# Attention mask: from a matmul into the score bank to a product after the exponential, with the sums one stage later

## The chip, the core and the metric

The kernel runs on one core of one Trainium2 chip. The metric is device time in microseconds (us) for one call; lower is better. One core has TensorE (matrix multiplies; PE in the profile, with its weight loads as PEld), VectorE (DVE), ScalarE (ACT), GpSimd (POOL), and DMA queues, here issued mostly by SyncE (SP). Every engine works through its own list of instructions in a fixed order and waits at an instruction until what it needs is there.

## The reference, cut to what matters

`y = scan_block(x, cond)` for 32 sequences of 256 tokens with 256 features, then two attention and feed-forward layers on `y`, then `x + result`. The part that the change touches is the local attention of each layer (8 heads of 64, window 128, so a sequence has two windows):

```python
sim  = jnp.einsum('bhwid,bhwjd->bhwij', bq, bk)          # q is already scaled
mask = (i < j) | (i > j + WINDOW) | (j == -1)
sim  = jnp.where(mask, -jnp.finfo(sim.dtype).max, sim)
attn = jax.nn.softmax(sim, axis=-1)
out  = jnp.einsum('bhwij,bhwjd->bhwid', attn, bv)
```

A masked score has weight zero; the rest is the exponential divided by its sum over the keys. Queries and keys are normalised to unit length, so the scores are bounded, and the kernel takes the exponential without subtracting a maximum (a second program in the file, for scales where that is not safe, is not run here).

## The kernel before

There are two kinds of work. The **scan** goes over the 256 tokens of eight sequences at a time (four groups): each of its 1024 steps is one custom VectorE instruction `h<-h,xrep,lim` (L660) that adds a scaled row to a state of 128x512 and clips it; TensorE reads the states out (`y`, L672), ScalarE scales the rows (`xrep`, L650), and chunks of 32 tokens have their own projection, convolution (`acc`, L442 on VectorE, first tap L431 on GpSimd), normalisation and output. The **attention and feed-forward** work goes over 64 items, one for each group, layer and sequence, in that order.

The two run side by side. For item n the program writes its steps into numbered stages, eight for an item (`ST = 8`); stage i of item n is entry 8n+i, and an entry of 8 or more falls into the time of the following items. The loop at the end emits the entries in order, and after each of them the scan steps that are due (`scan_to`): two for an entry, so one chunk of 32 scan steps goes with two items. A scheduler of the language then orders the instructions of each engine from this; `tc.keep_in_program_order` pins some of them. After the fourth group's scan has ended only attention and feed-forward are left.

What an item does, with the lines of the profile:

- `project` (L907): q, k, v of a window, two matmuls of 128x512 each; `rotated` works on q and k: square on ScalarE (L920), two products and a sum on VectorE (L923, L928, L933, L937), and on GpSimd an addition (L931), a power (L939) and a product (L940). This is done for the following item.
- `turn` (L946): transposes of q and k into `qT` and `kT`.
- `scores`: for keys of window `kw` and `n` pairs of heads, two PSUM banks `sc` of 128x512 (r is the head of the pair). Keys are the partitions, queries the columns. A bf16 matmul of an identity with a mask of 0 and -32768 (L1106) opens each bank; the score matmuls (L1113) accumulate onto it. ScalarE then writes the exponential into a tile `pT` (L1122; six buffers). Three calls an item: all four pairs against the second window's keys (`kw` 1, stage 2), and twice two pairs against the first window's keys (`kw` 0, stages 3 and 5). So an item has six banks, six mask matmuls and six exponentials.
- `sums` (L1132): the sums of `pT` over keys, 16 matmuls into one bank `rs`, and a reciprocal on VectorE (L1140). `values` (L1151): 16 matmuls of `pT` with `v_sb`, copied by ScalarE into `oT` (L1158). Both in stage 7.
- `put_inverse`, `load_inverse`: the reciprocal goes to DRAM and comes back spread over partitions (SyncE queue); `divide` multiplies `oT` with it (L1175); `finish` projects out (L957) and adds to the residual `res` (L965).
- `feed`: normalise (L1193 to L1203), `apply` (L1210), `spread` (L1223), `widen` (L1246, with a GELU L1254 on ScalarE), `product` (`ag`, L1262), `narrow` (L1274, with L1285).
- `fetch`: at the end of a layer the weights of the next one, on the SyncE queue.

All PSUM tiles are one rotation of eight banks (tag "w").

Of the kernel before, what the change touches and what calls it, by code (L numbers as in the profile page):

```python
# [10 lines left out]
FP = mybir.dt.float32  # L11
BF = mybir.dt.bfloat16
I32 = mybir.dt.int32
AF = mybir.ActivationFunctionType
ALU = mybir.AluOpType
# [4 lines left out]
P = 128  # L20
# [18 lines left out]
W = 128  # L39
# [4 lines left out]
LN_EPS = 1e-5  # L44
CLIP = 10.0
MASKED = -1e30
MASKED_LOW = -32768.0


SCALES2 = 25.0  # L50
# [2 lines left out]
def bc(ap, axis, n):  # L53

    ap = ap.unsqueeze(axis)
    shape = list(ap.shape)
    shape[axis] = n
    return ap.broadcast_to(shape)
# [15 lines left out]
def kernel(  # L74
# [29 lines left out]
    nc = tc.nc  # L104
# [4 lines left out]
    const = ctx.enter_context(tc.tile_pool(name="const", bufs=1))  # L109
# [35 lines left out]
    ident = const.tile([P, P], FP, tag="ident", name="ident")  # L145
# [17 lines left out]
    for j in range(NJ):  # L163
# [9 lines left out]
    nc.gpsimd.memset(half, 0.5)  # L173

    mask_t = const.tile([P, 2 * W], BF, tag="mask_t", name="mask_t")
    ident_b = const.tile([P, P], BF, tag="ident_b", name="ident_b")
    nc.vector.tensor_copy(ident_b, ident)
    nc.gpsimd.memset(mask_t, 0.0)  # L180
    nc.gpsimd.affine_select(
        out=mask_t[:, 0:W], in_=mask_t[:, 0:W], compare_op=ALU.is_ge, fill=MASKED_LOW,
        base=0, pattern=[[1, W]], channel_multiplier=-1,
    )
    nc.gpsimd.affine_select(
        out=mask_t[:, W : 2 * W], in_=mask_t[:, W : 2 * W], compare_op=ALU.is_ge,
        fill=MASKED_LOW, base=0, pattern=[[-1, W]], channel_multiplier=1,
    )

    head_cols = const.tile([P, 2, 32], FP, tag="head_cols", name="head_cols")  # L190
# [28 lines left out]
    def program(ctx, exact):  # L219
# [9 lines left out]
        ps_w = ctx.enter_context(tc.tile_pool(name="psw", bufs=8, space=PSUM, reuse_waits="tile"))  # L229
# [737 lines left out]
        if exact:  # L967

            mask = rpool.tile([P, 2 * W], FP, tag="mask", name="mask")
            nc.gpsimd.memset(mask, 0.0)  # L970
            nc.gpsimd.affine_select(
                out=mask[:, 0:W], in_=mask[:, 0:W], compare_op=ALU.is_ge, fill=MASKED,
                base=0, pattern=[[1, W]], channel_multiplier=-1,
            )
            nc.gpsimd.affine_select(
                out=mask[:, W : 2 * W], in_=mask[:, W : 2 * W], compare_op=ALU.is_ge, fill=MASKED,
                base=0, pattern=[[-1, W]], channel_multiplier=1,
# [94 lines left out]
        class Attention:  # L1072
# [2 lines left out]

            def __init__(self, l):
                self.l = l
                self.qkv, self.rot, self.p, self.o = {}, {}, {}, {}

            def project(self, b, w, a):  # L1080
                if w == 0 and a == 2:
# [16 lines left out]
            def scores(self, b, kw, i0, n):  # L1098


                qT, kT, _ = self.qkv[b]
                nq = S - kw * W
                banks = []
                for r in range(2):
                    sc = ps_w.tile([P, n, nq], FP, tag="w", name="sc")
                    nc.tensor.matmul(  # L1106
                        sc, ident_b, bc(mask_t[:, 0:nq], 1, n), start=True, stop=False
                    )
                    banks.append(sc)
                for i in range(n):  # L1110
                    for r in range(2):
                        rows = slice(r * DH, (r + 1) * DH)
                        nc.tensor.matmul(  # L1113
                            banks[r][:, i, :],
                            kT[rows, i0 + i, kw * W : (kw + 1) * W],
                            qT[rows, i0 + i, kw * W :],
                            start=False,
                            stop=(i == n - 1),
                        )
                for r in range(2):  # L1120
                    p = aw.tile([P, n, nq], FP, tag="pT", name="pT", bufs=6)
                    nc.scalar.activation(p, banks[r], AF.Exp)  # L1122
                    for i in range(n):
                        self.p[b, kw, i0 + i, r] = p[:, i, :]

            def sums(self, b):

                rs = bank(ps_w, "w", "rs")[:, 0:S]
                for kw in range(NW):
                    for r in range(2):  # L1130
                        for i in range(HEADS // 2):
                            nc.tensor.matmul(  # L1132
                                rs[32 * i : 32 * i + 32, kw * W :],
                                head_cols[:, r],
                                self.p[b, kw, i, r],
                                start=(kw == 0 and r == 0),
                                stop=(kw == NW - 1 and r == 1),
                            )
                rinv = aw.tile([P, S], FP, tag="rinv", name="rinv", bufs=1)
                nc.vector.reciprocal(rinv, rs)  # L1140
                self.rinv = rinv
# [155 lines left out]
        if exact:  # L1297
            for g in range(NG):
# [4 lines left out]
                for l in range(L):  # L1303
# [4 lines left out]
                    for b in range(GB):  # L1308
                        ff = FeedForward(g, l, b)
# [18 lines left out]
        def stage(n, i, what, *args):  # L1328
            stages.setdefault(ST * n + i, []).append(partial(what, *args))

        def attend(n, at, b, nxt):

            stage(n, 0, at.turn, b, 1)
            stage(n, 3, at.scores, b, 0, 0, 2)
            stage(n, 2, at.scores, b, 1, 0, HEADS // 2)
            stage(n, 5, at.scores, b, 0, 2, 2)
            stage(n, 7, at.sums, b)
            stage(n, 7, at.values, b)
            stage(n + 1, 0, at.put_inverse)
            stage(n + 1, 2, at.load_inverse)  # L1340
            stage(n + 1, 4, at.divide, b)
            stage(n + 1, 6, at.finish, b)
            if nxt is not None:
                for w in range(NW):
                    for i, a in ((0, 2), (1, 0), (1, 1)):
                        stage(n, 3 * w + i, nxt[0].project, nxt[1], w, a)
                stage(n, 6, nxt[0].turn, nxt[1], 0)

        def feed(n, g, l, b):
            ff = FeedForward(g, l, b)  # L1350
            for w in range(NW):
                stage(n + 1, 8 + w, ff.normalise, w)
                stage(n + 2, 1 + w, ff.apply, w)
                stage(n + 2, 2 + w, ff.spread, w)
            for m in range(NM):
                stage(n + 2, 4 + m, ff.widen, m)
                stage(n + 2, 5 + m, ff.product, m)
            for d in range(KM):
                stage(n + 3, 3 + d, ff.narrow, d)

        def fetch(n, g, l, b):

            if b == GB - 1 and (g, l) != (NG - 1, L - 1):
                nl = (l + 1) % L
                for i, a in ((5, 2), (6, 0), (6, 1)):
                    stage(n - 1, i, load_weights, nl, "qkv", a)
                stage(n + 2, 0, load_weights, nl, "wo")
                for m in range(NM):
                    stage(n + 2, 6 + m, load_weights, nl, "w1", m)
                stage(n + 3, 6, load_weights, nl, "w2")  # L1370
            if l == L - 1 and g < NG - 1:
                stage(n + 6, 2, load_res, g + 1, b)

# [2 lines left out]
        for n, (g, l, b) in enumerate(seqs):  # L1376
            nxt = (ats[n + 1], seqs[n + 1][2]) if n + 1 < len(seqs) else None
            attend(n, ats[n], b, nxt)
            feed(n, g, l, b)
        for n, (g, l, b) in enumerate(seqs):  # L1380
            fetch(n, g, l, b)
# [22 lines left out]
        for t in range(max(stages) + 1):  # L1404
# [3 lines left out]
            g, r = divmod(t + 1 + group - reload, group)  # L1408
# [10 lines left out]
    with tc.If(fits > 0) as which:  # L1419
        with ExitStack() as es:  # L1420
            program(es, False)
    with which.Else():
        with ExitStack() as es:
            program(es, True)
# [81 lines left out]
def _program(ins, out_shape):  # L1506
    import concourse.bacc as _bacc

    nc = _bacc.Bacc("TRN2", target_bir_lowering=False, num_devices=1)
    arrays, args = {}, []  # L1510
    for name, a in ins.items():
        arrays[f"in_{name}_dram"] = a
        args.append(
            nc.dram_tensor(
                f"in_{name}_dram", a.shape, mybir.dt.from_np(a.dtype), kind="ExternalInput"
            ).ap()
        )
    args.append(nc.dram_tensor("out_0_dram", out_shape, FP, kind="ExternalOutput").ap())
    with tile.TileContext(nc) as tc:
        kernel(tc, *args)  # L1520
    return nc, arrays
# [11 lines left out]
```

## Time and profile before

| | |
|---|---|
| time, median of 3 runs | 3769.12 us (3767.9 to 3770.96) |
| profiled execution, its own time | 3770.68 us |
| its span in the trace | 3768.9 us |
| granted TensorE clock, mean | 0.986 |
| busy in the span: PE / PEld | 3644.0 us (97%) / 2255.5 us (60%) |
| DVE / ACT / POOL | 2639.5 us (70%) / 2163.9 us (57%) / 1796.0 us (48%) |
| last scan step starts at | 2928.3 us |
| first mask matmul starts at | 515.1 us |

The span is the execution as the trace shows it; the profiled execution's own time is 1.8 us more than the span, and 1.6 us above the median. Busy time is a sum over the whole span, so an engine that is busy for 97% of it can still be waiting for another one in one stretch and be the limit in another. The first 480 us are scan alone; from there to about 2,930 us scan and attention run together; the last 840 us have no scan.

### The profile page before, as it was taken

Reading aid. Unit: us, or ns where it says so; the run is one execution under the profiler, and the core shown is the slowest. Engines: PE = TensorE matmul, PEld = TensorE weight load, DVE = VectorE, ACT = ScalarE, POOL = GpSimd, SP = SyncE. Lnnn points to the kernel's source line nnn. Section 1 sums busy time; section 2 is a strip of 40 time slices with the busy share of each in tenths; the row PEclk is TensorE's granted clock in tenths of the full one; section 3 lists DMA queues with packets and bytes.
Section 4 is the critical chain, followed back from the end, with each engine's and each line's share of the span. In section 5 each row is a group of like instructions: output and inputs, shape, how many; then the busy total and the mean of one; then the engine's idle time right before and its main releaser. Section 6 shows DMA issues by size and latency. Waiting matters only on the chain.

```text
span 3768.9 us, 57035 instructions
## 1 busy us (share of the span) xinstructions
PE 3644.0 (97%) x20028; PEld 2255.5 (60%) x20028; DVE 2639.5 (70%) x5177; ACT 2163.9 (57%) x3769; POOL 1796.0 (48%) x1776
## 2 busy tenths in 40 slices
PE   7999989999999999999999999999999999999998
PEld 3333345666666666666666666666666666666666
DVE  6988888788778777777777777777776444444443
ACT  3555556666666666656666665666566444444442
POOL 4443365544455455545445555545454444433441
PEclk8999999999999999999999999999999999999999
DMA  5444555344454545444444545444353111011101
GB/s 149 114 119 117 135 155 135 101 119 116 116 130 123 145 120 150 106 108 114 112 120 110 147 119 138 115 101 116 108 130 109 54 43 50 12 29 38 29 26 35
DMA packets 396250, 387.53 MB, mean 103 GB/s; under 512 B 176355, under 2 KB 256052, under 8 KB 395828
## 3 DMA queue, kind: packets, MB, share of 16 engines
q1 hardware_dynamic: 311506, 371.80, 37.1%
q10 hardware_dynamic: 84450, 12.01, 2.0%
q8 instruction: 161, 2.64, 0.3%
q14 instruction: 133, 1.09, 0.1%
HBM read 348.05 MB, written 34.08 MB: 101 GB/s over the span
## 4 chain that ended last, share of the span: by engine, by line
PE 68%; DVE 16%; POOL 6%; ACT 4%; issue 3%; DMA 3%; SPq 0%; ACTq 0%; POOLq 0%; DVEq 0%
PE ps_qkv L907 14%; PE pa L1246 13%; PE po_f L1274 8%; PE y L672 5%; DVE h L660 5%; PE ps_wo L957 4%; PE sc L1113 4%; PE ov L1151 3%; DVE acc L442 3%; PE ps_out L750 3%; PE ps_in L395 3%; PE tr_qk L946 2%; POOL rn L939 2%; PE rs L1132 2%; PE sc L1106 2%
## 5 line engine op out<-in xcount | busy, mean ns | idle before, releaser
L660 DVE CUSTOM_DVE_ANT_0 h<-h,xrep,lim 128x512 f32<-128x512 f32 x1024 | 936.5, 915 | 238.7 <-ACT xrep L650 207.7
L907 PE MATMUL ps_qkv<-qkv,res 128*128 128x512 f32 x1536 | 712.1, 600 | 23.6 <-DVE ag L1262 18.2
L650 ACT ACTIVATE xrep<-xrep,beta 128x512 f32<-128x512 f32 x896 | 622.5, 717 | 113.2 <-DMA xrep<-xnd 71.0
L1246 PE MATMUL pa<-hT,w 128*128 128x256 f32 (+1 forms) x3072 | 684.4, 385 | 0.3 <-DVE zT L741 0.2
L1246 PEld LDWEIGHTS pa<-hT,w 128*128 128x128 f32 (+1 forms) x3072 | 498.4, 178 | 159.6 <-issue 44.1
L931 POOL TENSOR_TENSOR rot<-rot,swp 128x512 f32<-128x512 f32 x256 | 335.2, 1309 | 368.9 <-DVE swp L928 223.7
L939 POOL TENSOR_TENSOR rn<-ss,neg_half 128x8 f32<-128x8 f32 x256 | 460.3, 1798 | 17.8 <-DVE ss L937 7.9
L907 PEld LDWEIGHTS ps_qkv<-qkv,res 128*128 128x128 f32 x1536 | 278.0, 191 | 300.5 <-issue 260.5
L1274 PE MATMUL po_f<-ag,w 128*128 128x256 f32 (+1 forms) x1536 | 386.8, 393 | 13.5 <-DVE ag L1262 8.9
L1203 POOL TENSOR_TENSOR rstd<-ve,neg_half 128x1 f32<-128x1 f32 x128 | 81.2, 634 | 645.7 <-DVE ve L1201 642.8
L672 PE MATMUL y<-h,ly 128*32 128x512 f32 x2048 | 372.7, 620 | 10.6 <-DVE h L660 9.8
L1274 PEld LDWEIGHTS po_f<-ag,w 128*128 128x128 f32 (+1 forms) x1536 | 273.0, 189 | 120.0 <-issue 54.6
L1262 DVE SCALAR_TENSOR_TENSOR ag<-pa,b_sb,ag 128x256 f32<-128x256 f32 (+1 forms) x448 | 212.5, 474 | 171.6 <-ACT ag L1254 168.0
L940 POOL TENSOR_TENSOR rot<-rot,rn 128x512 f32<-128x512 f32 x256 | 301.1, 1176 | 20.0
L1254 ACT ACTIVATE ag<-pa,b_sb 128x256 f32<-128x256 f32 x320 | 150.7, 471 | 268.1 <-PE pa L1246 266.0
L395 PE MATMUL ps_in<-xg,w_in_sb 128*128 128x256 f32 x1024 | 282.8, 407 | 19.1 <-DMA xg<-in_xT_dram 14.9
L920 ACT ACTIVATE sq<-ps_qkv 128x512 f32<-128x512 f32 x256 | 151.7, 596 | 236.5 <-PE ps_qkv L907 200.1
L395 PEld LDWEIGHTS ps_in<-xg,w_in_sb 128*128 128x128 f32 x1024 | 189.9, 198 | 142.4 <-issue 41.2
L442 DVE SCALAR_TENSOR_TENSOR acc<-xr,wc_sb,acc 128x256 f32<-128x256 f32 x384 | 189.5, 496 | 91.7 <-POOL acc L431 89.6
L923 DVE TENSOR_TENSOR rot<-ps_qkv,rc_sb 128x512 f32<-128x512 f32 x256 | 175.3, 685 | 82.9 <-ACT sq L920 82.9
L957 PE MATMUL ps_wo<-oT,wo 128*128 128x256 f32 x1024 | 231.6, 379 | 0.0
L450 ACT ACTIVATE th<-acc 128x256 f32<-128x256 f32 x128 | 53.0, 414 | 308.3 <-DVE acc L442 255.0
(146 smaller groups left out, 5672.4 us busy)
## 6 DMA issues: line engine op xcount, KB each, us to landing
xrep<-xnd SPq DMA_DIRECT2D x896, 256.0 KB
rb<-inv SPq DMA_DIRECT2D x128, 256.0 KB
xnd<-xn SPq DMA_DIRECT2D x64, 256.0 KB
qkv<-in_wqkv_dram SPq DMA_DIRECT2D x24, 512.0 KB
xd<-xnd SPq DMA_DIRECT2D x192, 64.0 KB
w<-in_w_dram SPq DMA_DIRECT2D x80, 128.0 KB
xg<-in_xT_dram SPq DMA_DIRECT2D x64, 128.0 KB
ys<-yo ACTq DMA_DIRECT2D x64, 128.0 KB
```

The costliest lines, as they stand in the source:

```text
L395: nc.tensor.matmul(ps, w_in_sb[:, k, ch * P : (ch + 1) * P], ck[c]["xg"][:, k], start=(k == 0), stop=(k == KM - 1),)
L442: nc.vector.scalar_tensor_tensor(acc, xr[:, :, k : k + CH], wc_sb[:, ch, k : k + 1], acc, ALU.mult, ALU.add,)
L650: scaled = nc.scalar.activation(bx, ck[c].pop(("bx", t), bx), AF.Copy, scale=ck[c]["beta"][:, t : t + 1])
L660: nc.vector._custom_dve(TENSOR_ADD_SAT, out=h_new, in0=state["h"], in1=bx, s0=ck[c]["lim"][:, 0, t : t + 1], s1=ck[c]["lim"][:, 1, t : t + 1],
L672: nc.tensor.matmul(ck[c]["y", hb][32 * q : 32 * q + 32, :], ly[hb % 2][:, 32 * t : 32 * t + 32], ck[c].pop(("h", hb * TB + t)), start=(i = ...
L907: nc.tensor.matmul(ps, res[b][:, k, t0 : t0 + W], wt["qkv", a][:, k], start=(k == 0), stop=(k == KM - 1),)
L931: nc.gpsimd.tensor_add(rot, rot, swp)
L939: nc.gpsimd.tensor_tensor(rn, ss, neg_half, ALU.pow)
L940: nc.gpsimd.tensor_mul(rot, rot, bc(rn, 2, DH))
L957: nc.tensor.matmul(po[:, d], wt["wo", 0][:, c, d * P : (d + 1) * P], oT[:, c, :], start=(c == 0), stop=(c == NC_ - 1),)
L1246: nc.tensor.matmul(pg if x else pa, wt["w1", m][:, k, x], self.h[:, k], start=(k == 0), stop=(k == KM - 1),)
L1274: nc.tensor.matmul(self.po[:, d], wt["w2", 0][r0 : r0 + n, m, d * P : (d + 1) * P], self.ag[m][r0 : r0 + n], start=(m == 0), stop=(m == le ...
```

## The change

The mask matmuls (`ident_b`, bf16 `mask_t`) are left out; each score matmul writes its own columns. `mask_t` becomes a float32 tile of ones and zeros, and a new step `mask` multiplies each `pT` tile of 128x512 in place with it: on GpSimd for `kw` 1 (two products an item, stage 3), on VectorE for `kw` 0 (two in stage 4 and two in stage 6). Each product is pinned in program order. `sums` and `values` move from stage 7 of an item to stage 0 of the following one, and all that comes after them for the item (the inverse's two transfers, divide, finish, the feed-forward steps, the fetches of wo, w1 and w2) moves by one stage too. The qkv fetches and the loading of the next group's residual stay.

```diff
--- before.py
+++ after.py
@@ -44,7 +44,6 @@
 LN_EPS = 1e-5
 CLIP = 10.0
 MASKED = -1e30
-MASKED_LOW = -32768.0
 
 
 SCALES2 = 25.0
@@ -173,18 +172,15 @@
     nc.gpsimd.memset(half, 0.5)
 
 
-
-    mask_t = const.tile([P, 2 * W], BF, tag="mask_t", name="mask_t")
-    ident_b = const.tile([P, P], BF, tag="ident_b", name="ident_b")
-    nc.vector.tensor_copy(ident_b, ident)
-    nc.gpsimd.memset(mask_t, 0.0)
+    mask_t = const.tile([P, 2 * W], FP, tag="mask_t", name="mask_t")
+    nc.gpsimd.memset(mask_t, 1.0)
     nc.gpsimd.affine_select(
-        out=mask_t[:, 0:W], in_=mask_t[:, 0:W], compare_op=ALU.is_ge, fill=MASKED_LOW,
+        out=mask_t[:, 0:W], in_=mask_t[:, 0:W], compare_op=ALU.is_ge, fill=0.0,
         base=0, pattern=[[1, W]], channel_multiplier=-1,
     )
     nc.gpsimd.affine_select(
         out=mask_t[:, W : 2 * W], in_=mask_t[:, W : 2 * W], compare_op=ALU.is_ge,
-        fill=MASKED_LOW, base=0, pattern=[[-1, W]], channel_multiplier=1,
+        fill=0.0, base=0, pattern=[[-1, W]], channel_multiplier=1,
     )
 
     head_cols = const.tile([P, 2, 32], FP, tag="head_cols", name="head_cols")
@@ -1075,7 +1071,7 @@
 
             def __init__(self, l):
                 self.l = l
-                self.qkv, self.rot, self.p, self.o = {}, {}, {}, {}
+                self.qkv, self.rot, self.p, self.ps, self.o = {}, {}, {}, {}, {}
 
             def project(self, b, w, a):
                 if w == 0 and a == 2:
@@ -1102,11 +1098,7 @@
                 nq = S - kw * W
                 banks = []
                 for r in range(2):
-                    sc = ps_w.tile([P, n, nq], FP, tag="w", name="sc")
-                    nc.tensor.matmul(
-                        sc, ident_b, bc(mask_t[:, 0:nq], 1, n), start=True, stop=False
-                    )
-                    banks.append(sc)
+                    banks.append(ps_w.tile([P, n, nq], FP, tag="w", name="sc"))
                 for i in range(n):
                     for r in range(2):
                         rows = slice(r * DH, (r + 1) * DH)
@@ -1114,14 +1106,25 @@
                             banks[r][:, i, :],
                             kT[rows, i0 + i, kw * W : (kw + 1) * W],
                             qT[rows, i0 + i, kw * W :],
-                            start=False,
-                            stop=(i == n - 1),
+                            start=True,
+                            stop=True,
                         )
                 for r in range(2):
                     p = aw.tile([P, n, nq], FP, tag="pT", name="pT", bufs=6)
                     nc.scalar.activation(p, banks[r], AF.Exp)
+                    self.ps[kw, i0, r] = p
                     for i in range(n):
                         self.p[b, kw, i0 + i, r] = p[:, i, :]
+
+            def mask(self, kw, i0):
+
+                e = nc.gpsimd if kw else nc.vector
+                for r in range(2):
+                    p = self.ps.pop((kw, i0, r))
+                    n, nq = p.shape[1:]
+                    tc.keep_in_program_order(
+                        e.tensor_mul(p, p, bc(mask_t[:, 0:nq], 1, n))
+                    )
 
             def sums(self, b):
 
@@ -1334,12 +1337,15 @@
             stage(n, 3, at.scores, b, 0, 0, 2)
             stage(n, 2, at.scores, b, 1, 0, HEADS // 2)
             stage(n, 5, at.scores, b, 0, 2, 2)
-            stage(n, 7, at.sums, b)
-            stage(n, 7, at.values, b)
-            stage(n + 1, 0, at.put_inverse)
-            stage(n + 1, 2, at.load_inverse)
-            stage(n + 1, 4, at.divide, b)
-            stage(n + 1, 6, at.finish, b)
+            stage(n, 3, at.mask, 1, 0)
+            stage(n, 4, at.mask, 0, 0)
+            stage(n, 6, at.mask, 0, 2)
+            stage(n + 1, 0, at.sums, b)
+            stage(n + 1, 0, at.values, b)
+            stage(n + 1, 1, at.put_inverse)
+            stage(n + 1, 3, at.load_inverse)
+            stage(n + 1, 5, at.divide, b)
+            stage(n + 1, 7, at.finish, b)
             if nxt is not None:
                 for w in range(NW):
                     for i, a in ((0, 2), (1, 0), (1, 1)):
@@ -1349,14 +1355,14 @@
         def feed(n, g, l, b):
             ff = FeedForward(g, l, b)
             for w in range(NW):
-                stage(n + 1, 8 + w, ff.normalise, w)
-                stage(n + 2, 1 + w, ff.apply, w)
-                stage(n + 2, 2 + w, ff.spread, w)
+                stage(n + 1, 9 + w, ff.normalise, w)
+                stage(n + 2, 2 + w, ff.apply, w)
+                stage(n + 2, 3 + w, ff.spread, w)
             for m in range(NM):
-                stage(n + 2, 4 + m, ff.widen, m)
-                stage(n + 2, 5 + m, ff.product, m)
+                stage(n + 2, 5 + m, ff.widen, m)
+                stage(n + 2, 6 + m, ff.product, m)
             for d in range(KM):
-                stage(n + 3, 3 + d, ff.narrow, d)
+                stage(n + 3, 4 + d, ff.narrow, d)
 
         def fetch(n, g, l, b):
 
@@ -1364,10 +1370,10 @@
                 nl = (l + 1) % L
                 for i, a in ((5, 2), (6, 0), (6, 1)):
                     stage(n - 1, i, load_weights, nl, "qkv", a)
-                stage(n + 2, 0, load_weights, nl, "wo")
+                stage(n + 2, 1, load_weights, nl, "wo")
                 for m in range(NM):
-                    stage(n + 2, 6 + m, load_weights, nl, "w1", m)
-                stage(n + 3, 6, load_weights, nl, "w2")
+                    stage(n + 2, 7 + m, load_weights, nl, "w1", m)
+                stage(n + 3, 7, load_weights, nl, "w2")
             if l == L - 1 and g < NG - 1:
                 stage(n + 6, 2, load_res, g + 1, b)
```

## The prediction

> **What bounds the kernel now.** I read the page's busy row and chain first, then the groups for prices, then the chain in order of time over one repetition of the work, then a table of windows cut where that chain changes engine.
>
> ```profile
> PE 3644.0 (97%) x20028; PEld 2255.5 (60%) x20028; DVE 2639.5 (70%) x5177; ACT 2163.9 (57%) x3769; POOL 1796.0 (48%) x1776
> PE 68%; DVE 16%; POOL 6%; ACT 4%; issue 3%; DMA 3%; SPq 0%; ACTq 0%; POOLq 0%; DVEq 0%
> ```
>
> PE is busy for 97%, yet carries only 68% of the chain. So there is time in which PE is busy and still not what sets the end. The page's groups price the products' neighbours; the answers for single lines give minimum, median and maximum.
>
> ```profile
> L660 DVE CUSTOM_DVE_ANT_0 h<-h,xrep,lim x1024: 707/810/1919, 54.3 to 2928.3; 128x512 f32<-128x512 f32 x171
> L923 DVE TENSOR_TENSOR rot<-ps_qkv,rc_sb x256: 672/683/694, 488.0 to 3666.8; 128x512 f32<-128x512 f32 x128
> L1175 DVE TENSOR_TENSOR oT<-oT,rb x64: 1214/1215/2291, 568.9 to 3724.0; 128x1024 f32<-128x1024 f32 x64
> L931 POOL TENSOR_TENSOR rot<-rot,swp x256: 1259/1272/1723, 489.4 to 3670.5; 128x512 f32<-128x512 f32 x128
> ```
>
> The chain repeats every two items (one chunk of the scan): the same `po_f` pair after a PE wait stands at 1543.69 and at 1652.26, 108.57 us apart. From 1543.69 to 1611.75 it is PE without a gap. Then it leaves PE (excerpt):
>
> ```profile
> 1610.02 1.73 PE ps_qkv L907 x4
> 1611.77 0.60 ACT sq L920
> 1612.40 0.69 DVE rot L923
> ...
> 1619.42 2.05 POOL rn L939
> ...
> 1622.55 1.27 POOL xd L702
> 1623.82 0.55 POOL acc L431
> 1624.39 0.48 DVE acc L442
> ...
> 1651.82 0.39 DVE ag L1262
> 1652.22 0.04 issue
> 1652.26 0.70 PE po_f L1274 x2
> 1652.96 0.37 PE tp_hn L1223 x2
> 1653.33 0.43 PE sc L1106 x2
> ```
>
> ```profile
> 1543.69:1611.75 68.06, 68.06 (x373) 43.44 (x374) 47.80 (x86) 42.36 (x75) 34.07 (x27) 1.00 0.44 114
> 1611.75:1652.26 40.51, 38.60 (x244) 25.32 (x244) 33.60 (x77) 25.20 (x44) 20.10 (x27) 1.00 0.32 85
> 2900.00:3300.00 400.00, 400.00 (x2270) 266.74 (x2269) 185.13 (x387) 192.27 (x311) 175.82 (x147) 1.00 0.15 41
> ```
>
> The columns are window, length, then busy PE, PEld, DVE, ACT, POOL. Of 108.57 us, 68.06 are a **PE stretch** (PE 100%, DVE 70%) and 40.51 a **VectorE stretch**: the convolution and the decays of the next chunk meet the rotations, DVE is busy for 33.60 us (83%), and PE idles only 1.91 us, because it has almost as much work. There a shorter PE gains nothing, and VectorE's time is the chain. In the last 840 us, without scan, PE is at 100% and DVE at 46%: the pure PE case.
>
> **What the Trainium skill says.** "SBUF — State Buffer", section "Who interferes with whom": a VectorE instruction with two SBUF inputs contends with a GpSimd instruction that reads SBUF, one with a single SBUF input does not. The trace agrees: `h` (two SBUF inputs) spreads from 707 to 1919 ns with a mean of 915, `rot` (one input from PSUM) stays within 672 to 694. Both new products have two SBUF inputs. "VectorE: DVE Perf Modes", the errata section, gives (N+151)/0.96 ns for a float32 tensor_tensor: 691 ns for 512 elements, and 1224 for 1024, where `oT` has 1215. "GPSIMD Engine Reference", "Engine selection", has two-input work about twice as slow on GpSimd: here 1272 against 683 ns.
>
> **The change part by part.**
>
> *Mask matmuls out.* The chain has 0.43 us for a pair, so 0.215 us each. Six an item, 64 items: 384 x 0.215 = 82.6 us of PE. Answers for L1106 by window find 128 of them after 2800 us, 250 from 560 to 2800, 6 before. After 2800 the chain is PE alone: 128 x 0.215 = **-27.5 us**, on the path. In a repetition, four pairs lie in the PE stretch (1544.76, 1561.93, 1595.83, 1600.71): -1.72 us; two lie in the VectorE stretch (1616.77, 1647.70): nothing. Their weight loads (98 ns) lie beside matmuls; nothing.
>
> *Products on VectorE*, 256 of 128x512. Not in the trace of before; bounded by 0.60 us (back-to-back `rot` in the chain) and 0.92 (`h`'s contended mean). I take 0.70, the skill's 691 ns. Per repetition eight, in four pairs. Two fall in the PE stretch, where DVE has 20 us to spare: nothing. The changed kernel's instruction order, as built, has the third just before the first `rot` of the VectorE stretch, where VectorE idled 0.81 and 1.35 us and where `divide` (1.22 us) moves away, to behind `zT`, into VectorE's 3.06 us wait for `acc` L431: nothing. It has the fourth between the `acc` steps that follow, where VectorE is the chain: +1.40 us. The repetition: -1.72 + 1.40 = -0.32. There are 250/12 = 20.8 of them: **-6.7 us**. If the cover is gone, each pair adds 1.2 to 1.84.
>
> *The new waits.* A product waits for its exponential. Queued behind it on VectorE are `h`, `acc` and `rot`, and all that waits for them; in the old trace the exponential of the fourth pair ends at 1619.8 and the place is about 1625, so I take no wait. Bounds: 0 to the 1.28 us table load before an exponential.
>
> *Products on GpSimd*, 128 of about 1.27 us, two an item at stage 3, so 2.5 us; behind them stand the rotations of the second window, for which `turn` waits. GpSimd was idle for 10.7 us before 1613.9, and without scan the last L940 ends at 3632.9 and its transposes begin at 3641.9: nothing. They do lock out `h` and the VectorE products while they run; from nothing up to 2.5 us for a repetition, if one pair meets the VectorE stretch. I take nothing, as the built order has them ahead of it.
>
> *One stage later.* `sums` comes three stages after its last exponential instead of two, so the product fits: 8 us lay between at 3627.6 to 3635.6, and 1.4 are needed. All its followers keep their spacing: the reciprocal, put_inverse and load_inverse (three DMAs an item on SP, each now behind about two more `xrep` loads in that queue, and SP waits there for the reciprocal as before), divide, finish. At seven layer ends 15 weight DMAs (wo, twelve w1, two w2) move by a stage too, with a stage of 5 to 7 us; their tiles come free as much later, so they are as far from their use. The v copy that reuses the buffer follows `values` on PE anyway; `pT` buffers come free more than 10 us before the next exponential of `kw` 1 needs them. All nothing. Only head and tail count: one stage without followers at the head, and one more of them at the end. A stage without scan is 41.57/8 = 5.2 us (the item period, 3607.93 to 3649.50); PE does the same work, so between 0 and 5.2: **+3 us**.
>
> Sum: -27.5 - 6.7 + 3 = -31.2. Against the profiled execution's 3770.68: 3739.5. That execution stands 1.56 above the median of the runs, so **3738 us**.
>
> **The rivals.**
>
> *PE limits everywhere* (the VectorE stretch dissolves because the work is realigned by a stage): 82.6 - 3 off, 3690. For it: PE's 97%. Against: 40 of every 108 us have their chain elsewhere.
>
> *The VectorE stretch grows* and the kernel is slower. Place: 1611 to 1652. Price: the third pair finds no idle time, both contended: 2 x 1.84 = 3.68, and the reciprocal (1751 ns), which ran beside a ScalarE chain at 1635.9 and stands a stage later in the new order, before `st` and `rot` that close the stretch: 1.75. Growth 5.43, less 1.72, times 20.8: +77; with -27.5 + 3: 3822. It decides from (27.5 - 3)/20.8 + 1.72 = 2.9 us of growth. For it: VectorE at 83% there with GpSimd locking; against: waits of 2 to 3 us in it that can absorb.
>
> *No change*: growth near 2.9, one pair and most of the reciprocal: 3769.
>
> *It does not do what it says*: the built order has 256 products on VectorE, 128 on GpSimd and no L1106 left. Excluded.
>
> **How the numbers follow.** A difference under 0.2% (7.5 us) can hardly be told from none. The forecast 0.42, its own range 3720 to 3757 (growth 0.5 to 2.3); PE everywhere 0.10; no change 0.13; slower 0.35. So faster 0.52, same 0.13, slower 0.35. For 8 in 10 the range runs from 3700, which leaves out the end of the PE case, to 3798, a growth of 4.3.
>
> **What would show it.** Right: item period without scan 41.57 - 6 x 0.215 = 40.3; PE busy near 3560; a repetition of about 108.2 with PE idle in it up from 1.9 to about 4.2; products on VectorE near 0.70. Wrong: PE waits at other places, a repetition over 109.8 (3822 needs 112.3) with VectorE gapless, or one near 106 with no stretch off PE.

## The result, and the profile after

The changed kernel is **slower: 3839.6 us** (median of 4 runs, 3832.06 to 3847.65) against 3769.65 us of the kernel before on the same chip, a ratio of **1.0182, 95% interval 1.0169 to 1.0195**. The forecast was 3738 us with a range up to 3798. The profiled execution has a span of 3845.9 us and a mean granted clock of 0.971, where the kernel before had 3768.9 us and 0.986.

The busy row and the chain of the page, kernel after:

```profile
PE 3636.3 (95%) x19644; PEld 2242.7 (58%) x19644; DVE 2881.8 (75%) x5432; ACT 2159.8 (56%) x3769; POOL 2005.2 (52%) x1904
...
PE 53%; DVE 22%; POOL 15%; issue 5%; ACT 3%; DMA 2%; SPq 0%; ACTq 0%; POOLq 0%; DVEq 0%
```

The 384 mask matmuls are gone (20028 to 19644), but PE's busy time fell by only 7.7 us instead of 82.6, and PE's share of the chain fell from 68% to 53%. The share that grew most is not VectorE's (16% to 22%), where the products are, but GpSimd's: 6% to 15%.

The products, and `h` beside them, by single line (minimum, median and maximum in ns, then when they run), kernel after:

```profile
L1126 DVE TENSOR_TENSOR pT<-pT,mask_t x256: 667/684/1769, 534.9 to 3778.1; 128x512 f32<-128x512 f32 x128
...
L1126 POOL TENSOR_TENSOR pT<-pT,mask_t x128: 1262/1280/1849, 530.8 to 3767.5; 128x512 f32<-128x512 f32 x128
...
L656 DVE CUSTOM_DVE_ANT_0 h<-h,xrep,lim x1024: 708/806/1929, 55.9 to 3004.8; 128x512 f32<-128x512 f32 x171
```

The median product costs what was priced, 684 ns on VectorE and 1280 on GpSimd; the means of the groups are higher, 830 and 1450 ns, because single products take up to 1769 and 1849. The mean of `h` is 917 ns, before 915.

One repetition of the work (two items, one chunk of the scan) in the table of windows, columns as in the prediction, cut where the chain returns to PE and where it leaves it again; and 400 us of which the first 105 still have the scan:

```profile
1946.33:1988.09 41.76, 41.76 (x241) 29.61 (x242) 31.50 (x53) 24.84 (x42) 20.98 (x16) 1.00 0.61 157
1988.09:2055.90 67.81, 64.63 (x365) 38.59 (x363) 55.56 (x117) 42.85 (x77) 39.59 (x43) 0.97 0.36 101
2900.00:3300.00 400.00, 390.95 (x2274) 260.94 (x2276) 247.98 (x453) 203.86 (x339) 202.47 (x166) 1.00 0.22 62
```

Before, 68.06 us of the 108.57 belonged to PE alone and 40.51 did not. Now 41.76 of 109.57 do and 67.81 do not. The PE stretch has lost 26 us, and those 26 us are now set by something else. Even in the 400 us listed last, PE is no longer at 100% as it was before: it idles for 9 us. The waits say for what. Columns: who waits for whom, total us, times, longest; kernel after, then kernel before:

```profile
DVE hn L1213 <- POOL rstd L1206: 223.1, 119, 4.5
...
PE tp_hn L1226 <- DVE hn L1213: 38.0, 35, 7.6
```

```profile
DVE hn L1210 <- POOL rstd L1203: 62.7, 102, 1.5
```

`rstd` is a power over 128x1, half a microsecond on GpSimd, two for an item: one for each window of the normalisation ahead of the feed-forward part. VectorE's wait for it grew from 62.7 to 223.1 us. The end of the repetition shown above, in the chain in order of time (start, us, what), kernel after:

```profile
2050.27 1.73 POOL rot L927
2052.00 1.62 POOL rn L935
2053.62 0.07 issue
2053.68 1.04 POOL rot L936
2054.73 0.52 POOL rstd L1206
2055.25 0.03 issue
2055.27 0.55 DVE hn L1213
2055.83 0.04 issue
2055.87 0.66 PE tp_x L490 x4
```

GpSimd finishes the rotations of q and k, only then takes the small power, VectorE's `hn` waits for that, and PE's next matmul waits until VectorE gets past `hn`. The timelines of a stretch without scan show the same with nothing around it. Columns: start us, us, engine, line, operation, and in brackets the idle time before it and what ended it. First GpSimd, then VectorE, then PE, all of the kernel after:

```profile
3309.14 0.55 POOL L1206 TENSOR_TENSOR rstd<-ve,neg_half 128x1 f32<-128x1 f32 x1 [15.97 <-DVE ve L1204]
3311.87 1.27 POOL L927 TENSOR_TENSOR rot<-rot,swp 128x512 f32<-128x512 f32 x1 [2.19 <-DVE swp L924]
3313.25 1.65 POOL L935 TENSOR_TENSOR rn<-ss,neg_half 128x8 f32<-128x8 f32 x1
3314.98 1.04 POOL L936 TENSOR_TENSOR rot<-rot,rn 128x512 f32<-128x512 f32 x1
3315.98 1.27 POOL L927 TENSOR_TENSOR rot<-rot,swp 128x512 f32<-128x512 f32 x1
3317.21 1.64 POOL L935 TENSOR_TENSOR rn<-ss,neg_half 128x8 f32<-128x8 f32 x1
3318.93 1.04 POOL L936 TENSOR_TENSOR rot<-rot,rn 128x512 f32<-128x512 f32 x1
3319.93 0.55 POOL L1206 TENSOR_TENSOR rstd<-ve,neg_half 128x1 f32<-128x1 f32 x1
```

```profile
3315.94 0.14 DVE L1204 TENSOR_SCALAR ve<-mv 128x1 f32<-128x1 f32 x1
3320.52 0.54 DVE L1213 TENSOR_SCALAR hn<-tp_h,mv,rstd 128x256 f32<-128x256 f32 x1 [4.44 <-POOL rstd L1206]
```

```profile
3317.00 2.95 PE L1277 MATMUL po_f<-ag,w 128*128 128x256 f32 x12
3321.21 0.41 PE L1226 MATMUL tp_hn<-ident,hn 128*128 128x128 f32 x2 [1.26 <-DVE hn L1213]
```

The power's input `ve` is complete at 3316.08 (3315.94 + 0.14). The power starts at 3319.93, because the rotations of q and k stand ahead of it: 3.85 us in a queue for 0.55 us of work. VectorE stands still for 4.44 us, PE for 1.26. An item saves six mask matmuls of 0.215 us, 1.29 us in all, and PE loses 1.26 of it here. So the item period without scan is 41.46 us, where it was 41.57: the gain is gone, but nothing is lost here (starts of `rs` in PE's timeline, kernel after):

```profile
3340.46 1.51 PE L1135 MATMUL rs<-pT,head_cols 128*32 128x256 f32 x32
...
3381.92 1.51 PE L1135 MATMUL rs<-pT,head_cols 128*32 128x256 f32 x32
```

The Trainium skill has the rule behind this, in "TensorE: Matmul & The Clock Gate", section "Architectural detail": VectorE, ScalarE and GpSimd take their queues strictly in order. The trace agrees, with those 3.85 us. Before the change both powers stood ahead of the rotations in GpSimd's timeline:

```profile
3601.53 0.55 POOL L1203 TENSOR_TENSOR rstd<-ve,neg_half 128x1 f32<-128x1 f32 x1 [9.48 <-DVE ve L1201]
3605.96 0.55 POOL L1203 TENSOR_TENSOR rstd<-ve,neg_half 128x1 f32<-128x1 f32 x1 [3.89 <-DVE ve L1201]
3608.50 1.27 POOL L931 TENSOR_TENSOR rot<-rot,swp 128x512 f32<-128x512 f32 x1 [1.98 <-PE sc L1106]
```

The program shows why. `normalise` of window 1 was entry 9 of item n + 1 (`stage(n + 1, 8 + w, ff.normalise, w)`), so it fell into the stage in which q and k of a first window are projected, and was emitted ahead of them there. One stage later it comes after them, and so does its power.

These stretches show the mechanism where it is plain, not where most of the time goes. By the starts of `rs`, the kernel after is 65.8 us behind the kernel before at item 16 already, 81.8 at item 44 and 78.3 at item 62. From item 16 to 44 a repetition takes 109.1 us in the mean, before 108.0.

### The profile page after: what moved, and what is told of

It reads as the page before. It is cut to its first block, busy times and chain, and to the rows that moved or that the text cites. A ratio compares the mean times of both kernels' runs of the same rounds, so it can differ in the third digit from the quotient of the medians.

```text
span 3845.9 us, 56772 instructions
## 1 busy us (share of the span) xinstructions
PE 3636.3 (95%) x19644; PEld 2242.7 (58%) x19644; DVE 2881.8 (75%) x5432; ACT 2159.8 (56%) x3769; POOL 2005.2 (52%) x1904
## 4 chain that ended last, share of the span: by engine, by line
PE 53%; DVE 22%; POOL 15%; issue 5%; ACT 3%; DMA 2%; SPq 0%; ACTq 0%; POOLq 0%; DVEq 0%
PE pa L1249 11%; PE ps_qkv L903 9%; DVE h L656 6%; PE po_f L1277 5%; POOL rn L935 5%; PE y L668 4%; PE ps_wo L953 4%; PE ov L1154 3%; POOL rot L936 3%; DVE acc L438 3%; PE ps_out L746 3%; POOL rot L927 3%; PE ps_in L391 2%; PE tr_qk L942 2%; DVE rot L919 2%
## 5 line engine op out<-in xcount | busy, mean ns | idle before, releaser
L903 PE MATMUL ps_qkv<-qkv,res 128*128 128x512 f32 x1536 | 742.6, 621 | 11.5 <-DMA res<-ys 4.4
L927 POOL TENSOR_TENSOR rot<-rot,swp 128x512 f32<-128x512 f32 x256 | 358.0, 1398 | 306.8 <-DVE swp L924 287.4
L1206 POOL TENSOR_TENSOR rstd<-ve,neg_half 128x1 f32<-128x1 f32 x128 | 72.2, 564 | 652.4 <-DVE ve L1204 650.9
L668 PE MATMUL y<-h,ly 128*32 128x512 f32 x2048 | 387.1, 623 | 25.4 <-DVE h L656 24.7
L1105 PE MATMUL sc<-qT,kT 64*128 64x128 f32 (+1 forms) x2048 | 239.5, 349 | 40.2 <-DVE swp L924 27.5
L438 DVE SCALAR_TENSOR_TENSOR acc<-xr,wc_sb,acc 128x256 f32<-128x256 f32 x384 | 202.8, 530 | 72.0 <-POOL acc L427 70.4
L1213 DVE TENSOR_SCALAR hn<-tp_h,mv,rstd 128x256 f32<-128x256 f32 x128 | 69.6, 543 | 223.2 <-POOL rstd L1206 223.1
L427 POOL TENSOR_SCALAR acc<-xr,wc_sb,bconv_sb 128x256 f32<-128x256 f32 x128 | 116.7, 912 | 230.0 <-DVE xr L421 203.6
```

The lines of the kernel that those rows point to most:

```text
L438: nc.vector.scalar_tensor_tensor(acc, xr[:, :, k : k + CH], wc_sb[:, ch, k : k + 1], acc, ALU.mult, ALU.add,)
L668: nc.tensor.matmul(ck[c]["y", hb][32 * q : 32 * q + 32, :], ly[hb % 2][:, 32 * t : 32 * t + 32], ck[c].pop(("h", hb * TB + t)), start=(i = ...
L903: nc.tensor.matmul(ps, res[b][:, k, t0 : t0 + W], wt["qkv", a][:, k], start=(k == 0), stop=(k == KM - 1),)
L927: nc.gpsimd.tensor_add(rot, rot, swp)
L1105: nc.tensor.matmul(banks[r][:, i, :], kT[rows, i0 + i, kw * W : (kw + 1) * W], qT[rows, i0 + i, kw * W :], start=True, stop=True,)
```

## The experiments

All twelve in one table (us, medians; the kernel before ran at 3770 beside each). The rows say how the mask is applied, the columns where the stages stand. "Norm ahead" has the later stages, but both normalisations in stage 9 instead of 9 and 10, so that both powers are emitted before the rotations.

| | old stages | later stages | later, norm ahead |
|---|---|---|---|
| mask matmuls | 3770 (before) | 3814 | 3781 |
| no mask | 3708 | 3787 | 3702 |
| GpSimd's products only | 3730 | 3805 | |
| VectorE's products only | 3752 | 3809 | |
| both products | 3773 | 3840 (after) | 3767 |

The twelfth, with matmuls for some items and products for others, stands at the end. Each ratio below has an interval of about 0.001 to 0.002 to either side, so that a difference of two cells is sure to some 9 us.

**The stages alone.** The kernel before with all that the change moves moved, and the mask matmuls kept:

```diff
-            stage(n, 7, at.sums, b)
-            stage(n, 7, at.values, b)
-            stage(n + 1, 0, at.put_inverse)
...
+            stage(n + 1, 0, at.sums, b)
+            stage(n + 1, 0, at.values, b)
+            stage(n + 1, 1, at.put_inverse)
...
-                stage(n + 1, 8 + w, ff.normalise, w)
+                stage(n + 1, 9 + w, ff.normalise, w)
```

> The kernel before with only the stages moved (sums, values and all that follows one stage later, wo/w1/w2 fetches too); mask matmuls kept, no products. Theory A (realignment: the second normalisation's power on GpSimd now stands behind the first window's two rotations, so hn and the transposes of hn come late): most of the loss is here although nothing was added, 3840 to 3920 us, and VectorE's wait for rstd grows from 63 us to some 220. Theory B (the products load the VectorE stretch): only head and tail, 3769 to 3780 us.

Measured: 3814.3 us, ratio 1.0124 (1.0108 to 1.0141). The shift by itself costs 44 us, with no product anywhere. That is more than theory B allows and less than the 3840 us that theory A asks for at least. Its group of `hn` (busy us, mean ns, then the idle time before it and what ended it) already has the whole wait:

```profile
L1210 DVE TENSOR_SCALAR hn<-tp_h,mv,rstd 128x256 f32<-128x256 f32 x128 | 69.5, 543 | 224.6 <-POOL rstd L1203 224.6
```

**The products alone.** The kernel after with the stages set back:

```diff
-            stage(n + 1, 0, at.sums, b)
-            stage(n + 1, 0, at.values, b)
+            stage(n, 7, at.sums, b)
+            stage(n, 7, at.values, b)
...
-                stage(n + 1, 9 + w, ff.normalise, w)
+                stage(n + 1, 8 + w, ff.normalise, w)
```

> The changed kernel with the old stages: products on VectorE and GpSimd, no mask matmuls, but sums and values in stage 7 and all followers where they were. Theory A: the predicted gain comes back, 3700 to 3750 us, item period without scan 40.3 us. Theory B: about as slow as the changed kernel, 3820 to 3850 us, VectorE without gaps in the scan part.

Measured: 3772.8 us, ratio 1.0011 (1.0004 to 1.0018), within 0.2% of before and between the ranges of the two theories: products for matmuls is an even exchange. The change's loss came with the stages, and `sums` did not need them: it fits two stages after the last exponential with the product between.

**No mask at all.** The kernel before without the mask matmuls and with nothing in their place:

```diff
-                    nc.tensor.matmul(
-                        sc, ident_b, bc(mask_t[:, 0:nq], 1, n), start=True, stop=False
-                    )
...
-                            start=False,
-                            stop=(i == n - 1),
+                            start=True,
+                            stop=True,
```

> The kernel before without the mask matmuls and without anything in their place (the scores are not masked); stages as before. It measures what the 82.6 us of TensorE are worth by themselves. TensorE as the limit everywhere: 3690 us. The two-stretch reading of the prediction (a gain only in the TensorE stretches and without scan: 27.5 + 20.8 x 1.72 = 63 us): 3706 us. If the work rearranges badly by itself: over 3740 us.

Measured: 3708.2 us, ratio 0.9840 (0.9823 to 0.9856): 62 us off, of the 82.6 that PE spends on them. It is the two-stretch reading that fits. In this window, which is wholly after the scan, PE has no idle time:

```profile
2900.00:3300.00 400.00, 400.00 (x2311) 271.47 (x2311) 184.81 (x394) 195.20 (x316) 180.19 (x151) 1.00 0.15 41
```

**The normalisations ahead.** The kernel after with one edit:

```diff
-                stage(n + 1, 9 + w, ff.normalise, w)
+                stage(n + 1, 9, ff.normalise, w)
```

> The changed kernel with one edit: both normalisations of an item in stage 9, so that both powers stand ahead of the first window's rotations in GpSimd's order. Theory A: item period without scan from 41.5 to 40.3 us, VectorE's wait for rstd back to some 60 us, total 3720 to 3780 us. Theory B: only the part without scan gains, 25 us, total 3800 to 3820 us.

Measured: 3766.9 us, ratio 0.9995 (0.9986 to 1.0004). 73 us come back from an edit that takes no work out. VectorE's wait for `rstd` is a third of what it was in the kernel before (62.7 us), so the edit does more than restore the old order. It moves the whole second normalisation (its transposes on PE and its statistics on VectorE too), not the power alone. Group of `hn`, and GpSimd's timeline, in which the two powers are one entry ahead of the rotations:

```profile
L1213 DVE TENSOR_SCALAR hn<-tp_h,mv,rstd 128x256 f32<-128x256 f32 x128 | 68.5, 535 | 20.7 <-POOL rstd L1206 20.7
```

```profile
3325.96 1.07 POOL L1206 TENSOR_TENSOR rstd<-ve,neg_half 128x1 f32<-128x1 f32 x2 [15.21 <-DVE ve L1204]
3328.73 1.27 POOL L927 TENSOR_TENSOR rot<-rot,swp 128x512 f32<-128x512 f32 x1 [1.71 <-DVE swp L924]
```

**The same edit without products.** The shift alone, with the normalisations ahead:

> Mask matmuls kept, sums and all that follows one stage later, and both normalisations of an item in stage 9, ahead of the first window's rotations on GpSimd. The stages alone cost 44 us (3814 us). If the second power behind the rotations is the whole of it: 3766 to 3780 us, and the first 16 items take no longer than in the kernel before. If the shift also meets the scan's chunks badly in the first 16 items: 3790 to 3810 us, with the loss there.

Measured: 3780.8 us, ratio 1.0023 (1.0013 to 1.0033). 33 of the 44 us of the shift come back, about 10 stay. The first 16 items do take longer than in the kernel before: `rs` of item 16 starts 21.6 us later. The wait is as short as with the products:

```profile
L1210 DVE TENSOR_SCALAR hn<-tp_h,mv,rstd 128x256 f32<-128x256 f32 x128 | 68.5, 535 | 21.0 <-POOL rstd L1203 21.0
```

**GpSimd's products alone, VectorE's products alone.** The old stages; from the run with products alone, two lines or one are taken out, so that the scores of `kw` 0 (first) or of `kw` 1 (second) stay without mask:

```diff
-            stage(n, 4, at.mask, 0, 0)
-            stage(n, 6, at.mask, 0, 2)
```

> Products at the old stages, GpSimd's alone: 128 products for the second window's keys; the scores of the first window's keys stay unmasked and there are no mask matmuls. Without any mask the time was 3708 us, with all products at the old stages 3773 us. Theory P1 (the loss of 65 us is VectorE's own time in the stretches that it limits): 3708 to 3725 us. Theory P2 (GpSimd's products delay the rotations behind them and lock VectorE out): 3745 to 3770 us.

```diff
-            stage(n, 3, at.mask, 1, 0)
```

> Products at the old stages, VectorE's alone: 256 products for the first window's keys; the scores of the second window's keys stay unmasked and there are no mask matmuls. Theory P1: 3750 to 3770 us. Theory P2: 3710 to 3730 us. By the prediction's price (1.40 us for a repetition of two items) it would be 3708 + 29 = 3737 us.

Measured: 3730.0 us (0.9892, 0.9875 to 0.9908) and 3751.6 us (0.9943, 0.9926 to 0.9961). Over the 3708 without mask, GpSimd's products cost 22 us and VectorE's 43; both cost 65, so the two costs add. VectorE's run is in the range of P1; GpSimd's lies between the two theories. What GpSimd's products take can be read at `h`, which no edit touched: groups of the run without mask, and of GpSimd's products alone:

```profile
L660 DVE CUSTOM_DVE_ANT_0 h<-h,xrep,lim 128x512 f32<-128x512 f32 x1024 | 932.9, 911 | 205.5 <-ACT xrep L650 176.1 <-DVE h L660 6.2 <-PE y L672 3.6
```

```profile
L656 DVE CUSTOM_DVE_ANT_0 h<-h,xrep,lim 128x512 f32<-128x512 f32 x1024 | 955.6, 933 | 194.8 <-ACT xrep L646 166.8 <-DVE h L656 6.4 <-PE y L668 2.1
```

The mean rises by 22 ns, over 1024 steps 22.7 us more of VectorE: the size of the loss. That the loss is these 22.7 us is not shown. No run slows `h` by itself, and with the later stages (next but one paragraph) the same products raise the mean of `h` from 892 to 924 ns, 33.6 us in all, for a loss of 17. VectorE's own products, in their group:

```profile
L1126 DVE TENSOR_TENSOR pT<-pT,mask_t 128x512 f32<-128x512 f32 x256 | 218.7, 894 | 0.0
```

They have a mean of 894 ns where 700 was priced, with no GpSimd product near; `h` is slower too, 920 against 911.

**The later stages without mask, and with either kind of products.** The kernel after, less all three `at.mask` lines, less the GpSimd one, less the two VectorE ones; the scores concerned stay without mask:

> The changed kernel without its products: no masking at all, sums and all that follows one stage later. Additive: 3708 (no mask) + 44 (stages, measured with the mask matmuls) = 3752 us. If the shift costs the same 67 us as beside the products (3840 - 3773): 3775 us.

> The changed kernel without GpSimd's products (scores of the second window's keys unmasked): later stages, VectorE's 256 products. Additive: 3752 + 44 = 3795 us. If the extra 23 us of shift and products together come from GpSimd's products queueing with the rotations and the second power: 3795 us here, and the 23 us in the other run. If they come from VectorE standing still at hn while its products queue behind: 3815 us here.

> The changed kernel without VectorE's products (scores of the first window's keys unmasked): later stages, GpSimd's 128 products. Additive: 3708 + 44 + 22 = 3774 us. If GpSimd's products and the second power in one queue make the extra 23 us: 3797 us.

Measured: 3787.3 (1.0048, 1.0032 to 1.0065), 3809.3 (1.0099, 1.0082 to 1.0115) and 3804.7 us (1.0090, 1.0073 to 1.0107). The first and the last are above both values expected for them, the second is between its two. With the later stages, taking the mask matmuls out gains 27 us (3814 to 3787), not 62. Part of the reason can be read in the waits from 3050 to 3650 us, without scan: PE waits there for `hn` for 19.3 us in all without mask and 17.7 us in the kernel after (1.3 us each time), but for 5.5 us where the mask matmuls are kept (0.4 us each time). VectorE's products cost 22 instead of 43, GpSimd's 17, both 52: here the two do not simply add, and what the other 13 us are is open.

**The later stages without mask, normalisations ahead.** The same single edit, on the kernel after without its three `at.mask` lines:

> No masking at all, sums and all that follows one stage later, and both normalisations in stage 9, ahead of the first window's rotations on GpSimd. Without the last edit 3787 us, with the old stages 3708 us. If the second power behind the rotations is what the shift costs: 3705 to 3720 us. If another 40 us of the shift have a different cause that the mask matmuls hid: 3745 us or more.

Measured: 3702.0 us, ratio 0.9818 (0.9802 to 0.9834), 6 less than with the old stages and below the range of 3705 to 3720. The later stages had cost 79 us without mask, and 85 come back. That the two are nearly equal is chance in part, as the table in the next section shows. The wait is again 20.6 us:

```profile
L1213 DVE TENSOR_SCALAR hn<-tp_h,mv,rstd 128x256 f32<-128x256 f32 x128 | 68.5, 535 | 20.6 <-POOL rstd L1206 20.6
```

**A mixture.** Old stages; items 0 to 43 keep the mask matmuls, items 44 to 63, the ones with little or no scan beside them, have the products (`FREE = 44`, and a bf16 product mask):

```diff
+                    if not self.free:
+                        nc.tensor.matmul(
+                            sc, ident_b, bc(mask_b[:, 0:nq], 1, n), start=True, stop=False
+                        )
...
+            if at.free:
                 stage(n, 3, at.mask, 1, 0)
                 stage(n, 4, at.mask, 0, 0)
                 stage(n, 6, at.mask, 0, 2)
```

> Old stages; mask matmuls for items 0 to 43, products on VectorE and GpSimd for items 44 to 63, which run without the scan (the product's mask as bf16). By the item periods measured without scan (41.57 us with matmuls, 40.28 with products at the old stages) 20 items gain 1.3 us each: 3744 us. If a product's wait or the mask's type costs anything: over 3755 us.

Measured: **3745.9 us, ratio 0.9936 (0.9920 to 0.9953)**: faster than both kernels, by 24 us against before. Starts of `rs` in PE's timeline:

```profile
3127.73 1.51 PE L1155 MATMUL rs<-pT,head_cols 128*32 128x256 f32 x32
3168.01 1.51 PE L1155 MATMUL rs<-pT,head_cols 128*32 128x256 f32 x32
3208.28 1.51 PE L1155 MATMUL rs<-pT,head_cols 128*32 128x256 f32 x32
```

An item takes 40.28 us: the 1.29 us of its mask matmuls are gained whole. Twenty items at 1.29 make 25.8, and 24 were gained.

## Why the prediction was wrong, point by point

*Mask matmuls out, about -63 (27.5 plus 1.72 for each of 20.8 repetitions).* **Right**, with the old stages: -62 with nothing in their place, and 35.5 of them by item 44 (the start of `rs`), where the working has 20.8 x 1.72 = 35.8 for the part with scan. The split of a repetition into a PE stretch and a VectorE stretch held. In the later stages the same step gives only -27: PE then waits for `hn` in part of the time that it gains.

*Later stages: "All nothing. Only head and tail", +3.* **This step failed: +44 with mask matmuls, +79 without, +67 with products.** The working looked at what moves, and found that every follower keeps its distance from what it follows. For GpSimd's queue it did not look at what does not move. `project` of the following item and `scores` stayed, so each moved step passed a different neighbour in each engine's queue. For the normalisation this put 8 us of rotations ahead of a 0.55 us power on GpSimd, and VectorE waits for that power with everything behind it. The three pairs with the normalisations ahead or not show that their place matters: 33, 85 and 73 us, in an edit of one number, with the wait going from about 224 to about 21 us each time. The wait is equally long in all three kernels, but where the mask matmuls are kept PE feels less of it (5.5 us against 19.3 and 17.7 in the 600 us above). One more reading made the step look safe: without scan PE was at 100% and VectorE at 46%, "the pure PE case"; but that VectorE has time to spare does not help when it stands still at `hn` and PE needs `hn`. The place of the second normalisation is not the whole of the step's cost; what is left is under "What stays open".

*Products on VectorE, +29 (one pair of four on the path, 1.40 us in a repetition).* **Mis-sized: +43.** The duration was too short: the forecast named 1.84 as the upper bound of a pair and took twice 0.70, though both inputs are in SBUF as with `h`, whose mean in the trace was 915. At the mean of 894 ns one pair gives 1.79 x 20.8 = 37. That this is near 43 does not make "one pair" right: in the chain of the run with VectorE's products alone, one repetition has two pairs, 2.28 us at 1999.27 and 2.29 us at 2016.71. How the 43 us divide between the longer products and the second pair is not separated.

*Products on GpSimd, nothing.* **Mis-sized: +22** with old stages, 17 later. The cover named was for GpSimd's own time, and held with the old stages: GpSimd's share of the chain is 7% with these products and without. What the products do to VectorE's instructions had a bound in the forecast (up to 2.5 us a repetition, 52 in all) and was set to zero; `h` became slower, but that the loss goes this way is not shown.

*New waits, nothing.* **About right**: the products on VectorE wait for their exponential for 17.3 us in the kernel after, and not at all with the old stages.

*The sum.* With the terms as measured, -62 + 43 + 22 = +3 for the products at old stages, as measured, and +67 for the stages: +70.

*The rivals.* The growing VectorE stretch (3822) had the right sign and nearly the right size, in part by luck. Its pieces are there: the chain of the repetition shown has two pairs of products (1.20 us each, at 2005.34 and 2020.50) and the reciprocal (1.67 us at 2034.88). But it put the whole loss into repetitions of 112.3 us, which measured 109.57; the kernel with the later stages and no product has 44 of the 70 us; and with the normalisations ahead, where the reciprocal stays in its later stage, the time comes back. "PE limits everywhere" was wrong: PE limits in less of the time than before.

*The signs named.* Item period 40.3: measured 41.46 in the kernel after; the mixture and its 40.28 show that the figure was right for the removal and the stages took it back. PE busy near 3560: measured 3636, see the last section. Repetition 108.2: measured 109.57 in the one shown, near the 109.8 named as wrong, and 109.1 in the mean from item 16 to 44.

**What stays open.** How much later than in the kernel before `rs` starts, in us, at items 16, 44 and 62 (each from one execution, a few us from the median of its kernel):

| | old stages | later stages | later, norm ahead |
|---|---|---|---|
| mask matmuls | 0, 0, 0 | 45.2, 39.4, 44.0 | 21.6, 17.5, 13.9 |
| no mask | -14.4, -35.5, -58.7 | 30.7, 20.9, 17.6 | 9.5, -41.3, -68.4 |
| both products | 15.5, 25.4, 2.1 | 65.8, 81.8, 78.3 | 35.3, 26.5, -0.9 |

In the first 16 items the later stages cost 45, 45 and 50 us, row by row. The normalisations ahead give back about half of that, and 20 to 24 us stay in every row. These are not explained; the items meet the chunks of the scan at another phase there, but no run varied that alone. From item 16 on it is the other way round: with the normalisations ahead the items run faster than with the old stages, by 8, 34 and 23 us up to item 62. So part of the 33, 85 and 73 us is a gain that the old stages did not have, and not the loss undone. No run has both normalisations in one stage with the old stages, so what that edit gains by itself is not known.

## What to carry to other kernels

When steps are moved by a stage, list for each in-order queue which instructions the moved ones pass, and look first at the shortest: a half-microsecond operation that lands behind eight microseconds of others becomes a stall for all that wait for it. That a group of steps keeps its internal distances proves nothing about its order against the steps that stay. A trade of one engine's time for another's is worth making only where the first engine is the limit: here in the items with little or no scan beside them (3746 us), not in all of them (3773).

## What the runs showed of the hardware that was not expected

PE's busy time isn't a measure of work. The run without mask, the later stages without mask, and the kernel after execute the same number of PE instructions; the busy rows of the first two, in this order:

```profile
PE 3574.1 (96%) x19644; PEld 2225.2 (60%) x19644; DVE 2642.3 (71%) x5177; ACT 2158.2 (58%) x3769; POOL 1822.7 (49%) x1776
```

```profile
PE 3604.3 (95%) x19644; PEld 2240.1 (59%) x19644; DVE 2644.0 (70%) x5176; ACT 2157.0 (57%) x3769; POOL 1800.9 (48%) x1776
```

Busy PE is 3574.1, 3604.3 and 3636.3 us, at mean granted clocks of 0.983, 0.978 and 0.971. So of the 136.9 us between the spans of the first and the last (3709.0 and 3845.9), 62.2 are the same matmuls, busy for longer. The clocks explain a large part of them: an estimate from the means (0.029 of 3845.9 us against 0.017 of 3709.0) is 48 us, or less where PE stood idle while its clock was low. The rest is not explained. So a stall of PE can be paid for twice, once as idle time and once at a lower clock after it. One such place, in the kernel before, as windows (the eighth column is the clock) and in PE's timeline:

```profile
604.00:608.64 4.64, 0.03 (x4) 0.03 (x1) 4.64 (x11) 0.66 (x3) 4.45 (x4) 0.94 0.04 15
608.64:616.00 7.36, 7.36 (x20) 3.77 (x21) 4.01 (x8) 2.91 (x6) 5.01 (x7) 0.57 0.22 62
616.00:624.00 8.00, 8.00 (x35) 3.98 (x34) 7.60 (x15) 7.16 (x13) 1.80 (x3) 1.00 0.47 132
```

```profile
608.64 0.66 PE L1223 MATMUL tp_hn<-ident,hn 128*128 128x128 f32 x2 [4.62 <-ACT th L450]
...
612.10 3.37 PE L907 MATMUL ps_qkv<-qkv,res 128*128 128x512 f32 x4
```

After 4.62 us of idling the mean clock is 0.57 for 7.36 us, and four `ps_qkv` matmuls take 3.37 us where they take 1.98 elsewhere. The Trainium skill, "TensorE: Matmul & The Clock Gate", section "Part 1: The HAM clock gate", has the clock at half after about 3.4 us of idling and full again after about as much sustained work. This trace agrees on the fall; the slow stretch lasted twice as long as that. On the idling, the kernel after decides against the page's figure: much less can be enough. Near the end of the repetition shown above PE waits for 0.85 and then 1.54 us (its matmuls start again at 2045.60 and 2047.80):

```profile
2045.66:2049.07 3.41, 1.87 (x9) 1.14 (x10) 3.41 (x9) 2.42 (x6) 3.33 (x4) 1.00 0.02 5
2049.07:2052.48 3.41, 3.41 (x8) 0.88 (x11) 2.14 (x6) 0.58 (x3) 3.41 (x3) 0.50 0.26 81
```

PE is busy for 1.87 of 3.41 us, more than half, and the next 3.41 us have a clock of 0.50, in which four `ps_qkv` matmuls take 3.58 us. From 1380 to 2830 us that trace has 14 such slow stretches of 3.4 or 6.8 us, about one in a repetition; in the kernel before the clock is 1.00 from 615 to 3750 us.
